# Softmax steps of an attention stage moved between engines, and embedding products that read their weights with a stride

## Chip, core and metric

The program runs on one core of a Trainium2 chip, as one launch. The core has five engines, each with its own queue in program order: TensorE (PE; its weight loads are listed apart as PEld), VectorE (DVE), ScalarE (ACT), GpSimd (POOL) and SyncE (SP), which issues DMAs. They wait for one another through semaphores. Matrix products land in PSUM, which GpSimd does not read in this kernel; everything else lies in SBUF. The metric is device time in microseconds, the median of several runs. All data are float32.

## What is computed

Four layers, each `x = x + layer(group_norm(x))`, on an input of 2 x 128 x 128 x 128 (batch, channel, height, width). The change is in layer 0, an axial attention along the height: each image column is a sequence of 128 positions, with 8 groups of channels. Cut to what matters:

```python
qr = einsum('bgci,cij->bgij', q, q_emb)
kr = einsum('bgci,cij->bgij', k, k_emb).swapaxes(2, 3)
qk = einsum('bgci,bgcj->bgij', q, k)
sim = bn(concat([qk, qr, kr])).reshape(NW, 3, 8, 128, 128).sum(axis=1)
sim = softmax(sim, axis=3)
sv  = einsum('bgij,bgcj->bgci', sim, v)
sve = einsum('bgij,cij->bgci', sim, v_emb)
out = bn(concat([sv, sve])).sum(...)      # sum of the two halves
```

`bn` normalises over batch and positions. There are 2 x 128 sequences and 8 groups, so 2048 matrices `sim` of 128 x 128. Layers 1 to 3 (scans, a deformable convolution, a convolution by 4 x 4 patches) are left as they are.

## The kernel before

The program prepares the statistics of layer 0 (`layer0_prepare`), then runs `layer0_attention`, merges the sums into the image (`Merge`), and then the other layers. The change is wholly in `layer0_attention`.

**Tiling.** The work is cut into 64 units: one image, one group, 32 image columns (`WC`). A unit is four *pairs* of two rows of four columns, that is 8 softmax matrices in a tile `e` of 128 x 1024: partition i is the query position, and the free axis holds 8 columns by 128 key positions. There are 256 pairs.

**Loop.** One loop over `m` (line 867) runs all pairs as a pipeline written out by hand. The `InOrder` helper (line 75) makes every engine keep the program's order, and all instructions that it issues carry line 83 in the profile, so that tiles tell them apart. Iteration `m` works on several pairs at once:

- `logits_pe` and `add_term` (pair m): PE turns the first term `r0` and adds the products `qk` into the PSUM tile `lg`; VectorE adds the second term `r1` and writes `e` (four buffers).
- `turn(e, 0)` and `turned` (pair m-2): PE transposes the first four matrices of a finished `e` into PSUM (`te`, one buffer); VectorE copies them into `et`. The second four follow near the end of the iteration.
- `maxima` (pair m): VectorE takes the negated row maxima into `mx`.
- `divide` (pair m-1): VectorE inverts the row sums `total`; GpSimd multiplies `e` by them, in place.
- `values` (pair m-3): PE multiplies `v` (as weights, `vt`) with `et`; ScalarE copies the result `po` to `svt`.
- `terms_pe` and `terms_copy`: PE makes a quarter of the next unit's terms in the PSUM tile `gen`; ScalarE scales and copies three quarters of it into `r`, VectorE the last quarter. Both write the same tile, ScalarE first.
- `embedded_pe` and `embedded_copy` (piece m-7): 32 products of value embeddings `ve` with the turned weights of one query position, for 32 columns at a time; ScalarE copies `po` to `ste`. The products go to four column groups of PE (output partitions 0, 32, 64, 96).
- `by_position` (pair m-2): GpSimd copies `et` (column, position) into the unit's tile `et2` (position, column), so that the 32 columns of one position lie side by side for these products. Both appear as `et` in the profile.
- `exponentials` (pair m): ScalarE runs one exponential for each of the 8 matrices, with the negated maximum as bias and the row sum accumulated on the way.
- `stats`: VectorE takes the statistics of `svt` and `ste`, at offsets of 7, 8, 11 and 14 iterations, each once per unit of four pairs.

[...] SyncE loads the next units (`load`, `load_qk`) and stores `svt` and `ste`, at fixed places of the loop.

A float32 product is recorded as two PE instructions, a transpose as one.

Of the kernel before, what the change touches and what calls it, by code (L numbers as in the profile page):

```python
# [7 lines left out]
F32 = mybir.dt.float32  # L8
I32 = mybir.dt.int32
AF = mybir.ActivationFunctionType  # L10
ALU = mybir.AluOpType
AX = mybir.AxisListType
# [3 lines left out]
P = 128  # L16
N = 2
S = 128
RT = 4
NT = S // RT  # L20
WC = 32
# [592 lines left out]
def layer0_attention(env, prm, mem, alphas, mv, then):  # L614
# [15 lines left out]
    pe, dve, act, pool, sync = (  # L630
        InOrder(tc, e) for e in (nc.tensor, nc.vector, nc.scalar, nc.gpsimd, nc.sync)
    )
    ident = env.ident
    HW = WC // 2
    with ExitStack() as ctx:
# [4 lines left out]
        tp = ctx.enter_context(tc.tile_pool(name="at_t", bufs=2))  # L640
        ep = ctx.enter_context(tc.tile_pool(name="at_e", bufs=3))
# [3 lines left out]
        st_v, st_e = (  # L645
            cp.tile([P, NG, N * NC, 2, 6], F32, name=f"st_so{k}", tag=f"st_so{k}")
            for k in range(2)
        )
# [49 lines left out]
        def terms_pe(u, t, k):  # L698

            if k == 0:  # L700
                u.r[t] = rp.tile([P, WC, S], F32, name=f"r{t}", tag=f"r{t}")
            ps = pp.tile([P, 4, 4, 4, WC], F32, name="gen", tag="gen")
            for b in range(4):
                for s in range(4):
                    pe.matmul(
                        ps[:, s, b],
                        lhsT=toep[32 * s : 32 * s + 32, t, 4 * k + b, :],
                        rhs=u.z[32 * s : 32 * s + 32, t, :, 4 * k + b, :],
                        start=True,
                        stop=True,  # L710
                    )
            return ps

        def terms_copy(u, t, k, ps, s):

            part = slice(0, 1) if s == 0 else slice(1, 4)
            to = u.r[t].rearrange("p w (s i) -> p s w i", s=4)
            to = to[:, part, :, 16 * k : 16 * k + 16]
            here = ps[:, part].rearrange("p s b i w -> p s w (b i)")
            scale = alphas[:, u.g, 1 + t : 2 + t]  # L720
            if s == 0:
                dve.tensor_scalar(to, here, scale, None, ALU.mult)
            else:
                act.activation(to, here, AF.Copy, scale=scale)

        def logits_pe(u, p):

# [26 lines left out]
        def add_term(u, p, lg):  # L754
            e = ep.tile([P, 2 * RT, S], F32, name="e", tag="e", bufs=4)
            dve.tensor_tensor(
                e,
                lg.rearrange("p r x j -> p (r x) j"),
                u.r[1][:, 2 * p * RT : 2 * (p + 1) * RT, :],
                ALU.add,  # L760
            )
            return e

        def maxima(e):
            mx = ep.tile([P, 2 * RT], F32, name="mx", tag="mx")
            dve.tensor_reduce(mx, e, AX.X, ALU.max, negate=True)
            return mx

        def exponentials(e, mx):
            total = ep.tile([P, 2 * RT], F32, name="total", tag="total")  # L770
            for w in range(2 * RT):
                act.activation(
                    e[:, w, :],
                    e[:, w, :],
                    AF.Exp,
                    bias=mx[:, w : w + 1],
                    accum_out=total[:, w : w + 1],
                )
            return total

        def divide(e, total):
            dve.reciprocal(total, total)
            pool.tensor_tensor(
                e, e, total.unsqueeze(2).to_broadcast([P, 2 * RT, S]), ALU.mult
            )
# [5 lines left out]
                pe.transpose(te[:, x, :], e[:, r * RT + x, :], ident)  # L791
            return te

        def turned(et, r, te):
            dve.tensor_copy(et[:, r * RT : (r + 1) * RT, :], te)

        def by_position(u, p, et):

            if p == 0:
                u.et = tp.tile([P, S, WC], F32, name="et2", tag="et2")  # L800
            lo = 2 * p * RT
            pool.tensor_copy(u.et[:, :, lo : lo + 2 * RT], et.rearrange("p w i -> p i w"))

        def values(u, p, et):

            for r in range(2):
                for x in range(RT):
                    pe.matmul(
                        po_v[32 * x : 32 * x + 16, r, :],
                        lhsT=u.v[:, (2 * p + r) * RT + x, :],  # L810
                        rhs=et[:, r * RT + x, :],
                        start=True,
                        stop=True,
                    )
            if p == 0:
                u.sv = sp.tile([P, 2 * RT, S], F32, name="svt", tag="svt")
            act.copy(u.sv[:, 2 * p : 2 * p + 2, :], po_v)

        def embedded_pe(u, k):

            for i in range(8 * k, 8 * k + 8):
                for s in range(4):
                    at = 32 * s + i
                    pe.matmul(
                        po_e[32 * s : 32 * s + 16, i % 8, :],
                        lhsT=ve[:, at, :],
                        rhs=u.et[:, at, :],
                        start=True,
                        stop=True,
                    )  # L830
# [24 lines left out]


        pairs = 4 * len(units)
        us, es, ets, totals = {}, {}, {}, {}
        for at in range(2):
            us[at] = load(at)  # L860
            load_qk(us[at])
        for t in range(2):
            for k in range(2):
                ps = terms_pe(us[0], t, k)
                for s in (0, 1):
                    terms_copy(us[0], t, k, ps, s)
        for m in range(pairs + 15):
            here = m < pairs
            if m == pairs:
                early.close()  # L870
                then()
            u, p = us.get(m // 4), m % 4
            nxt = us[m // 4 + 1] if m // 4 + 1 < len(units) else None
            turning = 0 <= m - 2 < pairs
            if here:
                lg = logits_pe(u, p)
                es[m] = add_term(u, p, lg)
            if turning:
                ub, pb = us[(m - 2) // 4], (m - 2) % 4
                e = es.pop(m - 2)  # L880
                et = ep.tile([P, 2 * RT, S], F32, name="et", tag="et", bufs=2)
                te = turn(e, 0)
                turned(et, 0, te)
            if here:
                mx = maxima(es[m])
            if m - 1 in totals:
                divide(es[m - 1], totals.pop(m - 1))
            if 0 <= m - 3 < pairs:
                values(us[(m - 3) // 4], (m - 3) % 4, ets.pop(m - 3))
            if nxt and here:  # L890
                ps = terms_pe(nxt, p // 2, p % 2)
                for s in (1, 0):
                    terms_copy(nxt, p // 2, p % 2, ps, s)
            piece = m - 7
            if 0 <= piece < pairs:
                embedded_pe(us[piece // 4], piece % 4)
                embedded_copy(us[piece // 4], piece % 4)
            if turning:
                te = turn(e, 1)
                turned(et, 1, te)  # L900
                by_position(ub, pb, et)
                ets[m - 2] = et
            if here:
                totals[m] = exponentials(es[m], mx)

            for st, k, half in ((st_v, 7, 0), (st_v, 8, 1), (st_e, 11, 0), (st_e, 14, 1)):
                if m >= k and (m - k) % 4 == 0 and (m - k) // 4 < len(units):
                    done = us[(m - k) // 4]
                    stats(done, st, done.sv if st is st_v else done.sve, half)
                    if half == 1 and done.n == N - 1 and done.wc == NC - 1:  # L910
                        k = int(st is st_e)
                        every = st[:, done.g].rearrange("p e f k -> p (e f k)")
                        dve.bn_aggr(mv[:, done.g, k, :], every)
            if m % 4 == 3 and m // 4 + 2 < len(units):
                us[m // 4 + 2] = load(m // 4 + 2)
            if m >= 4 and m % 4 == 0 and m // 4 + 1 < len(units):
                load_qk(us[m // 4 + 1])
            if m % 4 == 3 and m >= 7 and (m - 7) // 4 < len(units):
                store_sv(us[(m - 7) // 4])
            if m % 4 == 3 and m >= 11 and (m - 11) // 4 < len(units):  # L920
                store_sve(us[(m - 11) // 4])
            if m % 4 == 2 and m >= 14 and (m - 14) // 4 < len(units):
                us.pop((m - 14) // 4)
# [1286 lines left out]
```

## Time and profile before

| | us |
|---|---|
| median of 3 runs | 5367.43 (5363.36 to 5369.37) |
| profiled execution | 5362.39 |
| its span, first to last instruction | 5360.6 |
| first logits sum of attention | 424.8 |
| last logits sum of attention | 1893.3 |

Over the whole span PE is busy for 94%, VectorE 70%, ScalarE 50%, GpSimd 36%. These are averages over stages with different limits; the attention is the stretch from about 425 to 1925 us, and its own shares are shown below with the prediction. The costliest groups of the attention, by the page (busy us, mean ns of one):

| engine, tiles | form | count | busy | mean ns |
|---|---|---|---|---|
| ACT `e<-e,mx` exponential | 128x128 | 2048 | 793.4 | 395 |
| ACT accumulator read | 128x1 | 2048 | 396.3 | 194 |
| POOL `et<-et` | 128x1024 | 256 | 516.8 | 2019 |
| POOL `e<-e,total` | 128x1024 | 256 | 485.6 | 1897 |
| ACT `r<-gen,alphas` | 128x1536 | 256 | 395.0 | 1543 |
| DVE `et<-te` | 128x512 | 512 | 348.9 | 681 |

How to read it: `out<-in` names the tiles; a group's busy time is summed over all its instructions. On an engine whose queue is never empty, the recorded duration of an instruction overlaps the next one by some 0.1 us (0.07 on PE, 0.08 on VectorE), so a sum over a sequence is best made from start to start. Idle time in brackets is followed by what ended it.

### The profile page before, as it was taken

What the parts mean: (1) busy time and instruction counts of PE and PEld (TensorE: products, weight loads), DVE (VectorE), ACT (ScalarE), POOL (GpSimd) and SP (SyncE); (2) the same over time, 40 slices, a digit from 0 to 9 for tenths busy, and PEclk for the clock granted to TensorE, in tenths of its full rate; (3) what the DMA queues carried; (4) which work ended last, traced back from release to release, by engine and by line L of the source; (5) the groups of instructions that cost most, each with busy time, mean ns of one, the idle gap of its engine ahead of it and who ended that gap; (6) DMA issues with size and microseconds to landing.
All of it is one profiled execution on the core that took longest, in us unless ns stands there. A gap on an engine that the chain in (4) does not pass through costs nothing. (4 is left out here: it accounts for less than half of the span.)

```text
span 5360.6 us, 191912 instructions
## 1 busy us (share of the span) xinstructions
PE 5031.2 (94%) x82427; PEld 4370.6 (82%) x82427; DVE 3777.9 (70%) x7138; ACT 2677.6 (50%) x7974; POOL 1925.5 (36%) x1493
## 2 busy tenths in 40 slices
PE   7888999999999925999999999998999999999999
PEld 6757888888888815999999999996388888888777
DVE  3636888888888867555555556665478888888788
ACT  3557998888888845553223332001333333333322
POOL 3215666666666633000000001332023333333576
PEclk8998999999999967999999999999999999999999
DMA  4362333333333279940000000011311111111011
GB/s 164 123 254 56 60 59 61 62 61 60 58 61 62 55 302 273 84 49 1 1 2 1 1 1 17 33 48 51 124 43 32 33 31 37 32 33 32 32 52 56
DMA packets 509254, 348.41 MB, mean 65 GB/s; under 512 B 320884, under 2 KB 465780, under 8 KB 496496
## 3 DMA queue, kind: packets, MB, share of 16 engines
q1 hardware_dynamic: 503360, 326.50, 26.7%
q8 instruction: 655, 10.73, 0.8%
q10 hardware_dynamic: 5040, 9.55, 0.5%
q14 instruction: 199, 1.63, 0.1%
HBM read 194.97 MB, written 157.72 MB: 66 GB/s over the span
## 5 line engine op out<-in xcount | busy, mean ns | idle before, releaser
L83 PE MATMUL pl<-ln,wl 128*128 128x128 f32 (+1 forms) x10160 | 1241.6, 276 | 9.0 <-DVE ln L83 7.4
L83 PEld LDWEIGHTS pl<-ln,wl 128*128 128x128 f32 x10160 | 1176.4, 190 | 21.9 <-issue 6.2
L83 ACT ACTIVATE e<-e,mx 128x128 f32<-128x128 f32 x2048 | 793.4, 395 | 0.8 <-DVE mx L83 0.8
L83 POOL TENSOR_TENSOR w<-d 128x504 f32<-128x504 f32 x256 | 358.0, 1418 | 933.4 <-DVE s L83 738.7
L83 POOL TENSOR_TENSOR res<-ln,x1t 128x128 f32<-128x128 f32 x256 | 148.8, 582 | 1429.5 <-DVE ln L83 1429.5
L83 POOL TENSOR_TENSOR e<-e,total 128x1024 f32<-128x1024 f32 x256 | 485.6, 1897 | 486.8 <-DVE total L83 479.3
L83 ACT COPY res<-ln 128x64 f32<-128x64 f32 (+1 forms) x1016 | 284.1, 305 | 702.4 <-DVE ln L83 702.4
L83 PEld LDWEIGHTS ps_s<-s,xw 28*128 28x128 f32 x16384 | 526.2, 186 | 99.1 <-issue 63.0
L83 PE MATMUL ps_s<-s,xw 28*128 28x144 f32 x16384 | 582.1, 290 | 13.9 <-DMA xw<-px_d 11.3
L83 PE MATMUL po<-sm,wdef 128*128 128x256 f32 x2304 | 565.3, 391 | 0.0
L83 PE MATMUL pl<-ln,ws 128*128 128x128 f32 x4064 | 537.0, 273 | 0.0
L83 POOL COPY et<-et 128x1024 f32<-128x1024 f32 x256 | 516.8, 2019 | 37.1 <-DVE et L83 28.8
L83 DVE TENSOR_TENSOR v<-pl,c 128x128 f32<-128x128 f32 x508 | 148.2, 292 | 540.5 <-PE pl L83 537.3
L83 ACT COPY sm<-ps_s 128x576 f32<-128x576 f32 x512 | 301.1, 640 | 407.1 <-PE ps_s L83 407.1
L83 PEld LDWEIGHTS pl<-ln,ws 128*128 128x128 f32 x4064 | 494.8, 191 | 0.0
L83 PEld LDWEIGHTS po<-sm,wdef 128*128 128x128 f32 x2304 | 416.9, 190 | 83.4 <-issue 0.3
L83 ACT ACTIVATE r<-gen,alphas 128x1536 f32<-128x1536 f32 x256 | 395.0, 1543 | 172.1 <-PE gen L83 144.5
L83 ACT ACTIVATION_READ_ACCUMULATOR e<-e,mx 128x1 f32 x2048 | 396.3, 194 | 0.0
L83 DVE SCALAR_TENSOR_TENSOR ln<-v,res 128x128 f32<-128x128 f32 x1016 | 346.8, 341 | 48.5 <-POOL res L83 0.9
L83 PE MATMUL te<-cst_main,e 128*128 128x128 f32 x2048 | 337.6, 287 | 29.3 <-POOL e L83 20.4
L83 DVE STREAM_TRANSPOSE s<-w 128x1152 f32<-128x1152 f32 x256 | 349.6, 1366 | 16.0 <-PE ps_s L83 9.8
L83 DVE COPY et<-te 128x512 f32<-128x512 f32 x512 | 348.9, 681 | 14.0 <-PE te L83 13.4
(247 smaller groups left out, 8694.9 us busy)
## 6 DMA issues: line engine op xcount, KB each, us to landing
xw<-px_d SPq DMA_DIRECT2D x528, 56.0 KB
xa<-in_x SPq DMA_DIRECT2D x16, 1024.0 KB
v_d<-vs SPq DMA_DIRECT2D x16, 1024.0 KB
qb_d<-sb SPq DMA_DIRECT2D x16, 1024.0 KB
qa_d<-sa SPq DMA_DIRECT2D x8, 2048.0 KB
zz<-qb_d SPq DMA_DIRECT2D x1024, 16.0 KB
vt<-v_d SPq DMA_DIRECT2D x64, 256.0 KB
qk<-qa_d SPq DMA_DIRECT2D x256, 64.0 KB
```

What stands on the lines that cost most here:

```text
L83: return lambda *a, **k: self.tc.keep_in_program_order(issue(*a, **k))
```

## The change

Six edits in one function:

1. `terms_copy`: ScalarE copies the whole of `gen`; VectorE's quarter is gone.
2. `below_max` takes the place of `maxima`: VectorE takes the maxima (not negated), and GpSimd subtracts them from `e`, in place.
3. One exponential over all of `e`, without bias or accumulator, in place of eight.
4. `divide`: VectorE first sums the rows of `e`, then inverts, and GpSimd multiplies as before.
5. `turned` writes straight into a tile `et` of the whole unit, laid out (column, position); the first half of a pair is copied by ScalarE, the second by VectorE. The copy `by_position` is gone; `values` reads that tile, and `embedded_pe` reads one position of it, 32 columns at a stride of 128 elements.
6. The embedding products and their statistics come one iteration earlier (6, 10 and 13, where 7, 11 and 14 were).

```diff
-        def terms_copy(u, t, k, ps, s):
+        def terms_copy(u, t, k, ps):
...
-            if s == 0:
-                dve.tensor_scalar(to, here, scale, None, ALU.mult)
-            else:
-                act.activation(to, here, AF.Copy, scale=scale)
+            act.activation(
+                to[:, :, :, 16 * k : 16 * k + 16],
+                ps.rearrange("p s b i w -> p s w (b i)"),
+                AF.Copy,
+                scale=alphas[:, u.g, 1 + t : 2 + t],
+            )
...
-        def maxima(e):
+        def below_max(e):
             mx = ep.tile([P, 2 * RT], F32, name="mx", tag="mx")
-            dve.tensor_reduce(mx, e, AX.X, ALU.max, negate=True)
-            return mx
-
-        def exponentials(e, mx):
+            dve.tensor_reduce(mx, e, AX.X, ALU.max)
+            pool.tensor_tensor(
+                e, e, mx.unsqueeze(2).to_broadcast([P, 2 * RT, S]), ALU.subtract
+            )
+
+        def divide(e):
             total = ep.tile([P, 2 * RT], F32, name="total", tag="total")
-            for w in range(2 * RT):
-                act.activation(
-                    e[:, w, :],
-                    e[:, w, :],
-                    AF.Exp,
-                    bias=mx[:, w : w + 1],
-                    accum_out=total[:, w : w + 1],
-                )
-            return total
-
-        def divide(e, total):
+            dve.tensor_reduce(total, e, AX.X, ALU.add)
             dve.reciprocal(total, total)
...
-        def turned(et, r, te):
-            dve.tensor_copy(et[:, r * RT : (r + 1) * RT, :], te)
-
-        def by_position(u, p, et):
-
-            if p == 0:
-                u.et = tp.tile([P, S, WC], F32, name="et2", tag="et2")
-            lo = 2 * p * RT
-            pool.tensor_copy(u.et[:, :, lo : lo + 2 * RT], et.rearrange("p w i -> p i w"))
+        def turned(u, p, r, te):
+            if p == 0 and r == 0:
+                u.et = tp.tile([P, WC, S], F32, name="et", tag="et")
+            lo = (2 * p + r) * RT
+            (act.copy, dve.tensor_copy)[r](u.et[:, lo : lo + RT, :], te)
...
-                        rhs=et[:, r * RT + x, :],
+                        rhs=u.et[:, (2 * p + r) * RT + x, :],
...
-                        rhs=u.et[:, at, :],
+                        rhs=u.et[:, :, at],
...
                 te = turn(e, 0)
-                turned(et, 0, te)
+                turned(ub, pb, 0, te)
             if here:
-                mx = maxima(es[m])
-            if m - 1 in totals:
-                divide(es[m - 1], totals.pop(m - 1))
+                below_max(es[m])
+            if m - 1 in es:
+                divide(es[m - 1])
...
-            piece = m - 7
+            piece = m - 6
...
                 te = turn(e, 1)
-                turned(et, 1, te)
-                by_position(ub, pb, et)
-                ets[m - 2] = et
+                turned(ub, pb, 1, te)
             if here:
-                totals[m] = exponentials(es[m], mx)
-
-            for st, k, half in ((st_v, 7, 0), (st_v, 8, 1), (st_e, 11, 0), (st_e, 14, 1)):
+                act.activation(es[m], es[m], AF.Exp)
+
+            for st, k, half in ((st_v, 7, 0), (st_v, 8, 1), (st_e, 10, 0), (st_e, 13, 1)):
```

More of the change, by code (lines that the diff above doesn't have):

```diff
@@ L712, in terms_pe @@
             return ps
-        def terms_copy(u, t, k, ps, s):
-            part = slice(0, 1) if s == 0 else slice(1, 4)
+        def terms_copy(u, t, k, ps):
             to = u.r[t].rearrange("p w (s i) -> p s w i", s=4)
-            to = to[:, part, :, 16 * k : 16 * k + 16]
-            here = ps[:, part].rearrange("p s b i w -> p s w (b i)")
-            scale = alphas[:, u.g, 1 + t : 2 + t]
-            if s == 0:
-                dve.tensor_scalar(to, here, scale, None, ALU.mult)
-            else:
-                act.activation(to, here, AF.Copy, scale=scale)
+            act.activation(
[4 more added lines that the diff above has]
+            )
         def logits_pe(u, p):
@@ L792, in turn, with values @@
             return te
-        def turned(et, r, te):
-            dve.tensor_copy(et[:, r * RT : (r + 1) * RT, :], te)
-        def by_position(u, p, et):
-            if p == 0:
-                u.et = tp.tile([P, S, WC], F32, name="et2", tag="et2")
-            lo = 2 * p * RT
-            pool.tensor_copy(u.et[:, :, lo : lo + 2 * RT], et.rearrange("p w i -> p i w"))
-        def values(u, p, et):
+        def turned(u, p, r, te):
[3 more added lines that the diff above has]
+            (act.copy, dve.tensor_copy)[r](u.et[:, lo : lo + RT, :], te)
+        def values(u, p):
             for r in range(2):
@@ L857, in layer0_attention @@
         pairs = 4 * len(units)
-        us, es, ets, totals = {}, {}, {}, {}
+        us, es = {}, {}
         for at in range(2):
@@ L864, in layer0_attention @@
                 ps = terms_pe(us[0], t, k)
-                for s in (0, 1):
-                    terms_copy(us[0], t, k, ps, s)
+                terms_copy(us[0], t, k, ps)
         for m in range(pairs + 15):
@@ L880, in layer0_attention @@
                 e = es.pop(m - 2)
-                et = ep.tile([P, 2 * RT, S], F32, name="et", tag="et", bufs=2)
                 te = turn(e, 0)
-                turned(et, 0, te)
+                turned(ub, pb, 0, te)
             if here:
-                mx = maxima(es[m])
-            if m - 1 in totals:
-                divide(es[m - 1], totals.pop(m - 1))
+                below_max(es[m])
+            if m - 1 in es:
+                divide(es[m - 1])
             if 0 <= m - 3 < pairs:
-                values(us[(m - 3) // 4], (m - 3) % 4, ets.pop(m - 3))
+                values(us[(m - 3) // 4], (m - 3) % 4)
             if nxt and here:
                 ps = terms_pe(nxt, p // 2, p % 2)
-                for s in (1, 0):
-                    terms_copy(nxt, p // 2, p % 2, ps, s)
-            piece = m - 7
+                terms_copy(nxt, p // 2, p % 2, ps)
+            piece = m - 6
             if 0 <= piece < pairs:
```

## Prediction

> **What bounds the kernel now.** I began with the page: the change touches one stage only, so I looked for its place in the slices, and then for its first and last pair in the rows of the tile `e`. The columns are count, shortest/median/longest duration in ns, and first and last start in us.
>
> ```profile
> L83 DVE TENSOR_TENSOR e<-lg,r x256: 1160/1209/1226, 424.8 to 1893.3; 128x1024 f32<-128x1024 f32 x128
> L83 POOL TENSOR_TENSOR e<-e,total x256: 1894/1897/1900, 432.9 to 1906.0; 128x1024 f32<-128x1024 f32 x128
> ```
>
> There are 256 pairs, and the sum of two logit terms starts once in each: (1893.3 - 424.8) / 255 = **5.76 us per pair**. Every 0.1 us per pair is 25.6 us of the kernel.
>
> Next came the table by windows, to see which engine is full inside this stage (us, then busy us of PE, PEld, DVE, ACT, POOL with counts, granted clock, DMA share, GB/s).
>
> ```profile
> 700.00:1000.00 300.00, 293.43 (x7545) 246.96 (x7548) 258.01 (x366) 268.79 (x989) 203.01 (x104) 1.00 0.33 61
> 1000.00:1300.00 300.00, 292.48 (x7530) 246.26 (x7523) 257.81 (x366) 268.60 (x989) 203.02 (x104) 1.00 0.33 61
> ```
>
> PE is at 98%, at full clock; ScalarE 90%, VectorE 86%, GpSimd 68%, DMA a third. Busy PE alone proves little, since matmuls are pipelined, so I read one pair in PE's timeline and took distances from start to start.
>
> ```profile
> 1006.10 0.66 PE L83 MATMUL te<-cst_main,e 128*128 128x128 f32 x4
> 1006.59 1.04 PE L83 MATMUL lg<-cst_main,r 128*128 128x128 f32 x8
> 1007.56 1.16 PE L83 MATMUL lg<-qk 8*128 8x128 f32 x16
> 1008.65 0.65 PE L83 MATMUL te<-cst_main,e 128*128 128x128 f32 x4
> 1009.24 0.63 PE L83 MATMUL po<-et,vt 128*16 128x128 f32 x16
> 1009.80 1.17 PE L83 MATMUL gen<-zz,toep 32*128 32x128 f32 x32
> 1010.90 0.73 PE L83 MATMUL po<-et,ve 128*16 128x32 f32 x64
> 1011.56 0.65 PE L83 MATMUL te<-cst_main,e 128*128 128x128 f32 x4
> ```
>
> From one second `te` to the next, 1006.10 to 1011.56, is 5.46 us without a gap: 0.49 + 0.97 + 1.09 + 0.59 + 0.56 + 1.10 + 0.66. This is **PE's own round**. The stage runs 0.30 above it. Part of that is a second loop just below PE's round: logits, VectorE, GpSimd's division, then the first `te` of the next pair. VectorE and GpSimd around that pair:
>
> ```profile
> 1003.18 1.21 DVE L83 TENSOR_TENSOR e<-lg,r 128x1024 f32<-128x1024 f32 x1
> 1004.31 0.68 DVE L83 COPY et<-te 128x512 f32<-128x512 f32 x1
> 1004.90 1.21 DVE L83 TENSOR_REDUCE mx<-e 128x8 f32<-128x1024 f32 x1
> 1006.03 0.19 DVE L83 RECIPROCAL total<-total 128x8 f32<-128x8 f32 x1
> 1006.40 1.90 POOL L83 TENSOR_TENSOR e<-e,total 128x1024 f32<-128x1024 f32 x1 [1.29 <-DVE total L83]
> ```
>
> GpSimd divides the *previous* pair here, and its end (1008.30) releases that pair's first `te`, which stands after the next logits on PE (1008.65). From the end of logits: 0.05 (hand-over to VectorE) + 1.13 (sum) + 0.59 (copy) + 1.13 (maximum) + 0.20 (reciprocal) + 0.16 (hand-over to GpSimd; the rows show 0.14 and 0.18) + 1.90 + 0.05 = 5.21; logits' recorded end lies 0.07 past the point where the next PE instruction may start, so 5.28 against PE's 5.46. It is hidden by only 0.18, and when VectorE is late it isn't: weight loads of `te` waited 40.1 us for GpSimd's `e` (0.16 per pair). I carry the other 0.15 of the 0.30 (mostly "issue" gaps of PE) into the changed kernel.
>
> **The change, part by part (per pair).**
> *ScalarE.* Out: eight exponentials and eight accumulator reads, 1001.44 to 1004.53 in its timeline, 3.09. In: one exponential of 1024. The copies of 256 (364 ns) and 512 elements (586) give 0.87 ns per element over 0.14; so 1.03. The term copy grows from 1536 (1.54) to 2048 elements, 1.99; one turned half comes over, 0.59. With its two small copies and 0.1 of overlap for each of five: 1.03 + 1.99 + 0.59 + 0.36 + 0.36 - 0.5 = 3.83, where it was 1.44 + 0.25 + 3.09 + 0.26 = 5.04. ScalarE was not the bound, so this brings nothing by itself.
> *VectorE.* Out: the quarter of the term copy (0.67, and its wait for ScalarE's part: 160.0 us in 231 waits), and one turned half (0.59). In: the sum, at the price of the maximum, 1.13. From 4.93 to 4.80, and the four statistics of a unit fall on four different pairs, where two met on one (offsets 7 and 11 are both 3 modulo 4; now 7, 8, 10, 13). VectorE stays below PE; the gain is evenness.
> *GpSimd.* Out: the copy by position, 2.02. In: the subtraction, of the form of the division (two operands, one broadcast): 1.90, 1.84 from start to start. The load is the same, 3.7, but **the place is not**. The copy stood behind the division, and nobody waited for it within a pair. The subtraction waits for this pair's maximum and stands *ahead* of the previous pair's division. Queued behind it: that division; waiting for that: PE's first `te`, and behind it everything on PE. The loop is now 0.05 + 1.13 (sum of terms) + 1.21 (maximum, to its end) + 0.16 + 1.84 (subtraction) + 1.90 (division) + 0.05 + 0.07 = **6.41**. The reciprocal is ready at 0.05 + 3 x 1.13 + 0.20 + 0.16 = 3.80, before the subtraction has ended: the queue is the cause. 6.41 exceeds 5.46 by 0.95. That isn't paid each pair: if one `te` is 0.95 late, the next logits are late too, and the next division is then in time. Two pairs cost 6.41 + 5.46, so a pair costs 5.94.
> *Other new waits.* The exponential waits for the subtraction (done 4.45 after logits, exponential done 5.5); behind it is the copy of the next first `te`, which isn't there before 6.4 + 0.7. VectorE's sum of a pair waits for its exponential and blocks reciprocal, copy, statistics and the next sum of terms; it comes one pair later, at about 6.3 + 2.3 = 8.6 against 5.5. Both are covered by 1.6 us or more; uncovered, they would add to the 6.41.
> *Moved by one pair:* embedding products and their statistics. They still follow the last turned half of their unit by an iteration, PE's and SyncE's order of instructions is unchanged, DMAs too. Cost nothing.
> *PE.* The embedding products read 32 columns, each 512 bytes from the next, where they read neighbours. The trace has no such PE row. The floor is no cost; a gain is excluded, since the same 64 instructions read the same elements. The nearest rows are two copies of ScalarE, with the same stride in SBUF and without:
>
> ```profile
> L83 ACT COPY xc<-xa x64: 1052/1113/1135, 110.9 to 226.7; 128x512 f32<-128x512 f32 x64
> L83 ACT COPY xt<-ps_x x32: 586/586/592, 8.3 to 89.0; 128x512 f32<-128x512 f32 x32
> ```
>
> (1113 - 586) / 512 = 1.03 ns more per element. A pair streams 64 x 32 = 2048 elements per partition: 2.11 us if they pass one after another, 0.53 if four column groups run side by side. The products of `vt` speak for the latter: sixteen of 128 columns take 561 ns, 35 each, where the eight transposes of 128 columns take 121 each. I take **0.53**, and keep 0 and 2.11 as ends.
>
> [...]
>
> *Sum.* Two pairs: 6.41 + 5.46 + 0.15 + 0.53 = 12.55, a pair **6.28**, +0.52 x 256 = +133 us. Prologue and drain change by a microsecond or two. The profiled execution took 5362 us (span 5360.6); the median of the runs is 5 above it. 5362 + 133 + 5 = **5500**.
>
> **The rivals.**
> *The stride is free.* PE's moving operand may be fetched ahead; PE takes float32 more slowly than ScalarE in these rows (121 ns for 128 columns of a transpose, yet 35 side by side). Then (6.41 + 5.61) / 2 = 6.01, +64: 5431. Against it: ScalarE's stride pays in full. Chance 0.25.
> *One port for all four column groups.* The strided reads pass one after another: PE's round is 5.46 + 0.15 + 2.11 = 7.72, now above the GpSimd loop, which hides in it: +502, 5869. For it: 512 elements in 140 ns, as the `vt` products move them, may lie near what one port gives. Against: that is already faster than ScalarE's strided reads by far. Chance 0.22, with values between (1.0 gives PE 6.61, 5585) likelier than the end.
> *Faster: the subtraction is hidden, and VectorE's wait for ScalarE and the double statistics were what held PE up.* The place is GpSimd's queue; the point from which it decides is where (6.41 - 1.84 + s + 5.61) / 2 falls below 5.76, a subtraction s under 1.34 us, with a free stride. At s under 1.0 the loop vanishes behind PE's 5.61: -38, 5329. The division's 1894 to 1900 ns, whatever VectorE does beside it, speaks against. Chance 0.05.
> That the change doesn't do what it says can be left out: the planned order shows one exponential per pair, and subtraction ahead of division on GpSimd.
>
> **How the numbers follow.** The forecast has the remaining 0.48. Without the carried 0.15 and with a free stride it is 5.94, 5412; with 1.7 of stride 7.31, 5764. The range is 5410 to 5790, leaving out the port at its full price and the faster case. A change of 0.2% (11 us) is the least that a measurement of this kernel tells: faster 0.05, same 0.03, slower 0.92.
>
> **What would show it.** Right: the pair at about 6.3, first `te` waiting for GpSimd's `e` on PE with long and short pairs in turn, GpSimd's subtraction and division back to back, idle only before the subtraction; the burst of `ve` products at about 1.2 us from start to start, not 0.66; ScalarE and VectorE with more idle time. Wrong: a burst of 0.66 (free) or above 2 (one port); a subtraction much shorter than the division; PE waiting for ScalarE's exponential or VectorE's sum.

## The result, and the profile after

| kernel | median us | ratio to before (95% interval) |
|---|---|---|
| before | 5365.4 (4 runs) | 1 |
| changed | 5546.66 (4 runs, 5538.69 to 5547.64) | 1.0335 [1.0318, 1.0353] |

The change costs 181 us; the forecast was 5500, within 5410 to 5790. The profiled execution of the changed kernel has a span of 5545.6 us, 185 more than before. The rows of the tile `e` tell where (count, shortest/median/longest ns, first and last start):

```profile
L83 DVE TENSOR_TENSOR e<-lg,r x256: 1172/1225/1226, 427.5 to 2082.5; 128x1024 f32<-128x1024 f32 x128
L83 POOL TENSOR_TENSOR e<-e,mx x256: 1897/1947/2025, 430.2 to 2085.2; 128x1024 f32<-128x1024 f32 x128
L83 ACT ACTIVATE e<-e x256: 1045/1057/1091, 432.5 to 2087.2; 128x1024 f32<-128x1024 f32 x128
L83 POOL TENSOR_TENSOR e<-e,total x256: 1887/1898/1947, 436.2 to 2095.1; 128x1024 f32<-128x1024 f32 x128
```

The first row gives the pair: (2082.5 - 427.5) / 255 = 6.49 us, where it was 5.76. That is 0.73 x 256 = 187 us, so all of the loss lies in the attention. The next rows are the new subtraction at 1.95 us, the single exponential at 1.06 and the division, still at 1.90.

By windows (busy us of PE, PEld, DVE, ACT, POOL, then granted clock):

```profile
700.00:1000.00 300.00, 288.32 (x6701) 243.52 (x6694) 234.50 (x279) 196.32 (x231) 176.96 (x93) 1.00 0.30 56
1000.00:1300.00 300.00, 288.29 (x6642) 243.52 (x6643) 234.28 (x278) 196.49 (x233) 176.75 (x94) 1.00 0.27 53
```

ScalarE fell from 90% to 65% and VectorE from 86% to 78%: both have more idle time, as the change intends. PE is busy for 96% and gets fewer instructions done. Its timeline over two pairs shows both reasons:

```profile
1001.30 1.16 PE L83 MATMUL lg<-qk 8*128 8x128 f32 x16
1002.39 0.66 PE L83 MATMUL te<-cst_main,e 128*128 128x128 f32 x4
1002.97 0.63 PE L83 MATMUL po<-et,vt 128*16 128x128 f32 x16
1003.53 1.17 PE L83 MATMUL gen<-zz,toep 32*128 32x128 f32 x32
1004.64 1.35 PE L83 MATMUL po<-et,ve 128*16 128x32 f32 x64
1005.92 0.66 PE L83 MATMUL te<-cst_main,e 128*128 128x128 f32 x4
1006.42 1.04 PE L83 MATMUL lg<-cst_main,r 128*128 128x128 f32 x8
1007.38 1.16 PE L83 MATMUL lg<-qk 8*128 8x128 f32 x16
1009.06 0.66 PE L83 MATMUL te<-cst_main,e 128*128 128x128 f32 x4 [0.52 <-POOL e L83]
```

The burst of `ve` products lasts from 1004.64 to 1005.92, 1.28 us (before: 1010.90 to 1011.56, 0.66). And one first `te` starts at once behind its logits (1002.39), the next one waits for GpSimd's `e` (1009.06, which is 0.59 later than the queue would allow). The waits come in every second pair. VectorE and GpSimd between these two:

```profile
1002.57 1.22 DVE L83 TENSOR_TENSOR e<-lg,r 128x1024 f32<-128x1024 f32 x1 [0.75 <-PE lg L83]
1003.83 1.22 DVE L83 TENSOR_REDUCE mx<-e 128x8 f32<-128x1024 f32 x1
1004.97 1.21 DVE L83 TENSOR_REDUCE total<-e 128x8 f32<-128x1024 f32 x1
1006.22 0.20 DVE L83 RECIPROCAL total<-total 128x8 f32<-128x8 f32 x1
...
1005.22 1.93 POOL L83 TENSOR_TENSOR e<-e,mx 128x1024 f32<-128x1024 f32 x1 [3.08 <-DVE mx L83]
1007.10 1.91 POOL L83 TENSOR_TENSOR e<-e,total 128x1024 f32<-128x1024 f32 x1
```

The division's own input is there at 1006.22 + 0.20 = 1006.42; the division starts at 1007.10, right behind the subtraction. It is the queue that delays it, not the data.

### The profile page after: what moved, and what is told of

Read it like the earlier page. It is cut to its first block, busy times and chain, and to the rows that moved or that the text cites. A ratio compares the mean times of both kernels' runs of the same rounds, so it can differ in the third digit from the quotient of the medians.

```text
span 5545.6 us, 188136 instructions
## 1 busy us (share of the span) xinstructions
PE 5191.5 (94%) x82427; PEld 4511.2 (81%) x82427; DVE 3808.2 (69%) x6882; ACT 2438.6 (44%) x4390; POOL 1903.5 (34%) x1493
## 5 line engine op out<-in xcount | busy, mean ns | idle before, releaser
L83 PEld LDWEIGHTS pl<-ln,wl 128*128 128x128 f32 x10160 | 1176.0, 190 | 19.3 <-issue 4.7
L83 POOL TENSOR_TENSOR e<-e,mx 128x1024 f32<-128x1024 f32 x256 | 500.1, 1953 | 723.9 <-DVE mx L83 685.6
L83 ACT ACTIVATE r<-gen,alphas 128x2048 f32<-128x2048 f32 x256 | 518.4, 2025 | 237.8 <-PE gen L83 237.8
L83 DVE TENSOR_TENSOR e<-lg,r 128x1024 f32<-128x1024 f32 x256 | 313.5, 1225 | 223.5 <-PE lg L83 187.0
L83 PE MATMUL po<-et,ve 128*16 128x32 f32 x16384 | 349.8, 261 | 5.0 <-ACT svt L83 3.5
L83 PE MATMUL gen<-zz,toep 32*128 32x128 f32 x8192 | 334.6, 290 | 20.8 <-DMA zz<-qb_d 14.6
```

The costliest lines, as they stand in the source:

```text
L83: return lambda *a, **k: self.tc.keep_in_program_order(issue(*a, **k))
```

## The experiments

Two theories were to be told apart, and their sum: the **stride** lengthens PE's round (from 5.46 to about 6.10 us), and GpSimd's **queue** makes a loop of 6.67 us (from one first `te` to the next above, 1002.39 to 1009.06). Each of the two was taken out alone, then both, and the stride was put alone into the kernel before.

**Stride out.**

```diff
-                        rhs=u.et[:, :, at],
+                        rhs=u.et.rearrange("p w i -> p (w i)")[:, 32 * at : 32 * at + 32],
```

> The changed kernel with the stride alone taken out: the embedding products read 32 neighbouring elements of the same tile, as many as before (so they multiply other elements; the output of these products is not the reference's). Theory of two causes (the loop over GpSimd 6.67 us, PE's round 6.10 with the stride, 0.2 of stalls carried; a pair is half their sum): the burst of ve products goes back from 1.29 to 0.66 us, PE's round to 5.46, a pair to (6.67 + 5.46 + 0.2) / 2 = 6.17, so 0.32 x 256 = 82 us less than the changed kernel: about 5465, ratio to before 1.018. First te still waits for GpSimd. Rival, the stride is all of the loss: a pair loses the whole 0.63, 161 us, about 5385, ratio 1.004. Rival, the loop alone: no change, 5546, ratio 1.034.

Measured: 5623.64 us, ratio 1.0487 [1.0466, 1.0507]. The burst was back at 0.66 us from start to start, and yet the kernel lost another 77 us: all three expectations missed. PE's timeline, and below it the windows (busy PE, PEld, DVE, ACT, POOL, granted clock):

```profile
1010.11 1.16 PE L83 MATMUL lg<-qk 8*128 8x128 f32 x16
1012.38 1.08 PE L83 MATMUL te<-cst_main,e 128*128 128x128 f32 x4 [1.11 <-POOL e L83]
1013.39 1.05 PE L83 MATMUL po<-et,vt 128*16 128x128 f32 x16
1014.37 1.86 PE L83 MATMUL gen<-zz,toep 32*128 32x128 f32 x32
```

```profile
1009.00:1010.50 1.50, 1.50 (x17) 1.33 (x17) 1.47 (x4) 1.35 (x2) 1.50 (x2) 1.00 0.05 11
1010.50:1012.00 1.50, 0.77 (x14) 0.57 (x12) 1.03 (x2) 1.06 (x1) 1.50 (x1) 1.00 0.02 5
1012.00:1013.50 1.50, 1.12 (x8) 0.80 (x12) 1.47 (x2) 0.00 (x0) 0.32 (x1) 0.65 0.00 0
1013.50:1015.00 1.50, 1.50 (x28) 1.00 (x30) 1.49 (x2) 0.96 (x2) 0.97 (x1) 0.50 0.00 0
```

With PE's round shorter, its wait for GpSimd in every second pair grew to 1.11 us. Behind that wait the granted clock drops to 0.50, and the next products run slowly. From start to start `te`, `vt` and `gen` take 1.01 + 0.98 + 1.78 us (the last from the slow `gen` two pairs earlier, 1000.74 to 1002.52), where 0.59 + 0.56 + 1.11 is usual. That is 1.51 us more in two pairs, an estimated 193 us in 256. Together with a round of 5.46 and the loop, 6.65 in this run, it makes up the 13.63 us that two pairs take.

From 604.43 to 1533.25 us there are 69 slow `gen` bursts, 13.66 us apart on average, one in every two pairs: the loss repeats itself through the stage (mean clock 0.88 in every window from 500 to 1900 us). Why the clock falls behind a wait of 1.11 us, and what brings it back to 1.00 (before this wait, from about 1003 us on), was not shown.

**Queue out.** The division of a pair moves one iteration later and ahead of the next subtraction; turning and what follows move along.

```diff
-                below_max(es[m])
-            if m - 1 in es:
-                divide(es[m - 1])
+            if m - 2 in totals:
+                scale(es[m - 2], totals.pop(m - 2))
+            if here:
+                below_max(es[m])
+            if 0 <= m - 1 < pairs:
+                totals[m - 1] = divide(es[m - 1])
```

> The changed kernel with GpSimd's division of a pair one iteration later and ahead of the next subtraction; the turning, values, embedding products and statistics follow by one iteration, and e has five buffers. All is still computed. Nothing of a pair then waits for the subtraction within the same round. Theory of two causes: the pair falls to PE's round with the stride, 6.10 + 0.1 to 0.2, about 6.25, so 61 us less than the changed kernel: about 5485, ratio 1.022. Rival, the stride is all of the loss: the same time as the changed kernel, 5546, ratio 1.034, with PE waiting somewhere else. Rival, the loop alone (the stride hidden): back to 5.6 to 5.7 per pair, about 5340, ratio 0.995.

Measured: 5461.6 us, ratio 1.0184 [1.0163, 1.0205]. PE is busy throughout, and its round with the stride (6.10 us from second `te` to second `te`, 1003.02 to 1009.12 in its timeline) is the bound:

```profile
1000.00:1300.00 300.00, 300.00 (x7027) 255.27 (x7025) 246.02 (x291) 206.54 (x243) 183.01 (x97) 1.00 0.30 56
```

**Both out.**

> Both edits together: division one iteration later, and 32 neighbouring elements read (the embedding products multiply other elements). Theory of two causes: PE's round of 5.46 + 0.1 to 0.2, a pair at 5.6 to 5.66, so 0.85 x 256 = 218 us less than the changed kernel: about 5330, ratio 0.993, under the kernel before, since VectorE's wait for ScalarE and the double statistics are gone. Rival, something else in the change costs time (ScalarE's longer term copy, the sum on VectorE): a pair stays above 5.76 and the time above 5365.

Measured: 5316.81 us, ratio 0.9912 [0.9894, 0.9931]. No other part of the change shows a cost: without its two costs this kernel is 47 us under the kernel before. The kernel before was not run with a late division, so it stays open how much of the 47 us is due to the change. From here, the stride alone is 5461.6 - 5316.8 = 145 us, and the queue on top of the stride 5546.7 - 5461.6 = 85 us. The order matters: the queue without the stride is 5623.6 - 5316.8 = 307 us, of which the estimate above puts 193 down to the clock.

**Was it the clock?** The kernel with the stride out was given useless work where PE waits:

```diff
             te = pp.tile([P, RT, S], F32, name="te", tag="te")
+            for x in range(3 if r == 0 else 0):
+                pe.matmul(te[:, x % RT, :], lhsT=ident, rhs=ident, start=True, stop=True)
```

> The kernel a_neighbours (changed kernel, neighbours read, early division; 5624 us with TensorE's granted clock at 0.88 in the attention) with three useless products of the identity, about 0.7 us in each pair, issued on PE after the logits and ahead of the first te, where PE waits for GpSimd; their result is overwritten. Theory that the lost clock made that run slow: the filler takes the place of the idle time, the clock stays at 1.00, and a pair is (6.67 + 5.46 + 0.73 + 0.2) / 2 = 6.53, about 5555, ratio 1.036: more work, and some 70 us less. Rival, the clock is lost for another reason or doesn't matter: the time stays at 5624 or rises by up to 0.7 x 256 / 2 = 90 us.

Measured: 5484.77 us, ratio 1.0219 [1.0203, 1.0234], clock 1.00 in the attention, PE busy throughout:

```profile
1000.00:1300.00 300.00, 300.00 (x7150) 259.74 (x7151) 242.29 (x288) 197.65 (x240) 179.38 (x97) 1.00 0.30 56
```

More work made the kernel 139 us faster. The time was 70 us under the expectation, which put the filler into PE's round once. It stands between logits and first `te` in both pairs that the loop spans, so the loop's 6.67 meets 5.46 + 2 x 0.77 = 7.00 of PE's work and is hidden altogether; the pair is PE's round, 5.46 + 0.77, with stalls 6.26.

**Only exchanging the two GpSimd instructions.**

```diff
-                below_max(es[m])
+                mx = below_max(es[m])
             if m - 1 in es:
                 divide(es[m - 1])
+            if here:
+                subtract(es[m], mx)
```

> The changed kernel with only the two GpSimd instructions of an iteration exchanged: division of the previous pair first, then the subtraction of this one. All is still computed. If the queue's order alone were the price, the division would end 1.9 us earlier, the pair would fall to PE's round, about 6.25, 5485, ratio 1.022. My theory says that this only moves the loop: division, subtraction, exponential, sum, reciprocal and the next division then follow one another in every iteration, 1.90 + 1.90 + 0.06 + 1.06 + 0.06 + 1.25 + 0.20 + 0.17 = 6.6 us per pair without any pair in between being spared, so about 0.1 x 256 = 28 us more than the changed kernel: 5575, ratio 1.039.

Measured: 5641.34 us, ratio 1.0522 [1.0502, 1.0541]: slower, as expected, but by 95 us and not 28. ScalarE's and PE's timelines show what my loop left out:

```profile
1007.13 1.06 ACT L83 ACTIVATE e<-e 128x1024 f32<-128x1024 f32 x1 [3.11 <-POOL e L83]
1008.09 0.57 ACT L83 COPY et<-te 128x512 f32<-128x512 f32 x1
1008.55 0.38 ACT L83 COPY svt<-po 128x256 f32<-128x256 f32 x1
...
1008.98 1.36 PE L83 MATMUL po<-et,ve 128*16 128x32 f32 x64 [1.07 <-ACT svt L83]
```

The exponential waits for the late subtraction, and behind it in ScalarE's queue stand the copies of `te` and of `svt`; PE's `ve` products wait for the latter (127.2 us in 170 waits between 500 and 1900 us). A wait that is moved off one queue lands on the next one.

This run also bears on the clock. Waits of 1.0 to 1.1 us come in every second pair here too, some 13.7 us apart (at 609.04, 622.81, 636.55 us and on), and the longest is 1.4 us; yet the clock stays at 1.00:

```profile
1000.00:1300.00 300.00, 271.56 (x6300) 228.51 (x6288) 221.28 (x262) 175.49 (x219) 161.98 (x87) 1.00 0.27 51
```

So neither the length of a wait nor the idle share of PE (9% here, 8% with the stride out) decides alone. These waits stand between `gen` and `ve`, the others between the products of 8 rows and the transposes `te`; whether that is the difference was not tried.

**The stride in the kernel before.** First with the embedding products left in their place:

```diff
-            pool.tensor_copy(u.et[:, :, lo : lo + 2 * RT], et.rearrange("p w i -> p i w"))
...
+            dve.tensor_copy(u.et[:, lo : lo + RT, :], te)
...
-                        rhs=u.et[:, at, :],
+                        rhs=u.et[:, :, at],
```

> The kernel before with the stride alone: VectorE copies both turned halves into a tile of the whole unit by column, GpSimd's copy by position is gone, and the embedding products read 32 columns at a stride of 512 bytes. Softmax steps as before. All is still computed. Theory of two causes: PE's round grows from 5.46 to 6.10 and hides all that is shorter; a pair at 6.10 + 0.05 to 0.15, about 6.2, so 0.44 x 256 = 113 us more: 5476, ratio 1.021. Rival, the stride costs only where something else holds PE up as well: under 30 us, ratio under 1.006.

Measured: 5607.07 us, ratio 1.0452 [1.0436, 1.0468]. Something else was slow; VectorE's waits named it (us in total, times, longest):

```profile
DVE et L83 <- PE po L83: 112.8, 50, 2.3
```

The tile of a unit has two buffers. VectorE now writes the first half of a unit's first pair straight into one, while in the same iteration PE's last products of the unit two before still have to read it. The clock has a share in the loss as well: with such a wait PE stood still for 0.81 us (for VectorE's `et`) and 0.68 us (for GpSimd's `e`) within one round, both the means of 50 waits between 500 and 1850 us, and in the attention the mean granted clock was 0.95 to 0.96. The same kernel with the products one iteration earlier, as in the change:

```diff
-            piece = m - 7
+            piece = m - 6
```

> The kernel b_stride (kernel before with the stride; 5607 us) with the embedding products one iteration earlier, at 6 as in the changed kernel, and their statistics at 10 and 13. All is still computed. In b_stride VectorE waited 112.8 us in 50 waits, 2.3 us each at the start of a unit, for the products to leave the unit's tile, which has two buffers. If that is what b_stride had on top, the wait is gone, PE's round of 6.10 bounds the pair as in a_late_division (6.14 to 6.19), and the time is about 5476, ratio 1.021. Rival, the strided products themselves cost more here than in the changed kernel: the time stays near 5607.

Measured: 5468.64 us, ratio 1.0194 [1.0177, 1.0211]; the wait is gone, and the clock is 1.00 again. So the stride costs 104 us in the old order of steps, with the statistics moved as in the change (worth 7 us, below), and the shift by one iteration is part of the stride's price, not decoration.

**Which strides cost.** In the kernel with the late division, every second or fourth element was read. Either any stride costs the same, or the cost grows with the distance.

```diff
-                        rhs=u.et[:, :, at],
+                        rhs=u.et.rearrange("p w i -> p (w i)")[:, at : at + 63 : 2],
```

> The kernel a_late_division (5462 us, 32 columns 512 bytes apart, burst of 64 products 1.29 us) with the 32 columns taken every second element, 8 bytes apart (other elements are multiplied). [...] If any stride costs, the burst is at 1.29 and the time 5462.

With every fourth element, 16 bytes apart, and a cost of the stride that may grow with the distance:

> [...] If it grows with the distance, the burst lies between 0.66 and 1.29 us: about 5320 to 5400.

The bursts at 8 and at 16 bytes (the second number is recorded, 0.07 longer than from start to start):

```profile
1006.18 0.74 PE L83 MATMUL po<-et,ve 128*16 128x32 f32 x64
1004.41 1.14 PE L83 MATMUL po<-et,ve 128*16 128x32 f32 x64
```

From start to start in PE's timelines:

| distance of elements | burst us | kernel us | ratio to before |
|---|---|---|---|
| 4 bytes | 0.66 | 5316.8 | 0.9912 [0.9894, 0.9931] |
| 8 bytes | 0.67 | 5311.3 | 0.9901 [0.9882, 0.9921] |
| 16 bytes | 1.07 | 5406.1 | 1.0078 [1.0058, 1.0098] |
| 512 bytes | 1.29 | 5461.6 | 1.0184 [1.0163, 1.0205] |

Eight bytes are free (0.67 us against 0.66), so not every stride costs. Sixteen are not: 1.07 us lies between 0.66 and 1.29, as a cost that grows with the distance would have it, and 5406 us is 6 above the range given for that. Why the cost sets in between 8 and 16 bytes, and where the 0.22 us between 16 and 512 come from, stays open.

**The statistics alone.**

```diff
-((st_v, 7, 0), (st_v, 8, 1), (st_e, 11, 0), (st_e, 14, 1))
+((st_v, 7, 0), (st_v, 8, 1), (st_e, 10, 0), (st_e, 13, 1))
```

> The kernel before with one edit of the change alone: the embedding statistics at offsets 10 and 13 (they were 11 and 14), so that no pair has two statistics on VectorE. All is still computed. If VectorE's uneven load was behind a part of the 0.30 us by which a pair of the kernel before stood above PE's round, the pair falls by about 0.1: 28 us less, 5335, ratio 0.995. Rival: PE's own stalls are all of it, no change, 5364, ratio 1.000.

Measured: 5358.15 us, ratio 0.9987 [0.998, 0.9994]: a gain of 7 us, a quarter of what was expected. PE's waits for GpSimd's `e` in mid-stage (500 to 1850 us) went from 9.9 us to 4.6, but its "issue" gaps before `po` stayed (16.2 before, 19.3 now).

**A version that beats both.** Late division, and the stride given to ScalarE, which copies each half out of PSUM a second time by position:

```diff
-                u.et = tp.tile([P, WC, S], F32, name="et", tag="et")
+                u.et = tp.tile([P, S, WC], F32, name="et2", tag="et2")
...
-            (act.copy, dve.tensor_copy)[r](u.et[:, lo : lo + RT, :], te)
+            (act.copy, dve.tensor_copy)[r](u.now[:, r * RT : (r + 1) * RT, :], te)
+            act.copy(u.et[:, :, lo : lo + RT], te.rearrange("p x i -> p i x"))
```

> A version that computes everything and should beat both: the changed kernel with the division one iteration later (as in a_late_division), and without the stride on PE. ScalarE copies each turned half out of PSUM a second time, by position (runs of 4 written 128 bytes apart), into the tile that the embedding products read, so they read 32 neighbours; the values read a small tile by column as in the kernel before. ScalarE gets two copies of 512 more, about 0.5 us each: 3.8 + 1.0 = 4.9 us per pair, under PE's 5.46. Theory of two causes: the same pair as a_late_neighbours, 5.57 us, about 5320, ratio 0.992. Rival: writes with a stride cost ScalarE 1.03 ns more per element, as its strided reads do, so 1.0 us each; ScalarE then takes 5.9 us per pair and bounds it: 5400 to 5420, ratio 1.008.

Measured: 5345.61 us, ratio 0.9965 [0.9951, 0.9978], 20 us under the kernel before. The rows of `et` show the copies:

```profile
L83 ACT COPY et<-te x768: 568/587/601, 439.0 to 1904.1; 128x512 f32<-128x512 f32 x192
```

All 768, with and without scattered writes, take 0.57 to 0.60 us: writing runs of 16 bytes, and reading PSUM at a distance, costs ScalarE nothing here. The rival falls. The time is 29 us above that of both costs taken out; "issue" gaps of PE (15.5 us before `po` in mid-stage, where both costs out leave 4.1) lie beside it, but what causes them was not tried.

## Why the prediction was right

*The bound.* PE's round was the bound before, with the loop over GpSimd just below it. That the round lengthens with the stride (always busy with the late division) and that the loop then rises above it (PE waits in every second pair) are both seen.

*The loop.* Forecast 6.41, measured 6.67. In the rows above, from the end of logits (1001.30 + 1.16 = 1002.46) to the first `te` at 1009.06, plus 0.07: 0.11 + 1.26 + 1.22 + 0.17 + 1.88 + 1.91 + 0.05 + 0.07. The largest miss is the sum of terms: 1.13 from start to start before, when a copy of another tile stood behind it; now the maximum of the same tile follows, and starts only after the sum's end (1002.57 + 1.22 = 1003.79), 1.26 later. The division, at 1.90, was right.

*The burst.* Forecast +0.53, measured +0.63 (0.66 to 1.29). The row it was taken from, ScalarE's strided copy, and the assumption that four column groups run side by side gave the right size; a single port for all at ScalarE's price (+2.11) and a free stride are excluded. The size is in part luck. No run tested that ScalarE's price per element holds on PE, or that the groups run side by side: 0.63 us over 2048 elements is as well 0.31 ns for each of them in a row.

*Half of the sum.* Two pairs were to cost the loop and one PE round. Measured, 2 x 6.49 = 12.98 = 6.67 + 6.10 + 0.21. The stalls carried over were put at 0.15 for the two; 0.21 is left.

*The stalls.* The forecast took 0.16 of the 0.30 per pair for the loop, from 40.1 us that weight loads waited. PE's products themselves waited only 20.4 us for `e`, 0.08 per pair. The rest is found in `gen`: once per unit its burst takes some 1.45 us from start to start, where 1.10 is usual. In mid-stage that adds 21 us over 222 bursts before and 19 us over 193 after, 0.10 per pair in both kernels, so 0.20 for two pairs. The carried 0.15 came near it without having found it. What lengthens this burst was not tried.

A pair came out 6.49 - 6.28 = 0.21 above the forecast, 54 us (47 between the forecast and the median). These terms make it up: 0.26 in the loop, 0.10 in the burst and 0.06 in stalls, 0.42 for two pairs.

*Costs put at nothing.* The exponential, the sum on VectorE and the longer term copy: right as far as the time shows, since both costs out gives less than before. The shift by one iteration: nothing in the change, but 138 us where it is missing in the old order (5607.07 against 5468.64, a part of it by the clock), and the forecast didn't see that it was needed. The evenness of VectorE was named as a gain; alone it is worth 7 us.

*The rivals.* "The stride is free" would have made the kernel faster than it is by the forecast's sum (5431). The run without the stride shows that this sum could not have held: it left out that PE's clock falls behind the longer wait. The faster case needed a subtraction under 1.34 us; it takes 1.95.

## What to carry to other kernels

An instruction that is moved to an idle engine takes a place in that engine's queue (85 us here, on top of the stride): look at what stands behind it, and at who waits for that, before counting the load. Taking a copy away in favour of a strided read moved its cost to the reader here: GpSimd's copy (2.02 us) was off the critical path, and PE's read (0.63 us more per pair) is on it. Two costs on one loop didn't add up (the queue cost 85 us with the stride and 307 without it): repair them together, and look at the granted clock when a repair makes things worse (it was 0.88 with the stride alone taken out).

## What the runs showed of the hardware

- PE's moving operand paid for strides of 16 bytes and more: 32 columns of float32 in four column groups, 64 products in 0.66 us at 4 bytes, 0.67 at 8, 1.07 at 16 and 1.29 at 512.
- Behind a wait of 1.11 us on PE, in every second pair, the granted clock was halved for about a quarter of the time (mean 0.88), and a filler of 0.77 us brought back 1.00. The length of the wait alone does not decide: with two waits of 0.81 and 0.68 us within one round, 50 times each, the mean was 0.95 to 0.96, while waits of 1.0 to 1.4 us left the clock at 1.00 with the two GpSimd instructions exchanged. What decides stays open.
- While PE read at 512 bytes, other engines were slower too: GpSimd's subtraction took 1.95 us in the changed kernel (1.94 with the late division) and ScalarE's term copy 2.03 (2.02), where they took 1.90 and 1.97 at distances of 4, 8 and 16 bytes. The cause was not tried.
- ScalarE read PSUM at a distance of 512 bytes and wrote SBUF in runs of 16 bytes at 0.59 us for 512 elements, the same as without, while its read of SBUF at 512 bytes takes 1.11 (the copies `xc` ahead of the attention).
